# Storing x early and adding the attention output in DRAM, in a two-layer graph kernel on one core

## The chip, the cores and the metric

The kernel runs on one core of one Trainium2 chip. The metric is the device time of one execution in microseconds (us). The engines are PE (matrix products; PEld is its weight load), DVE (vector), ACT (scalar), POOL (GpSimd) and SP, which here only issues transfers. All arrays are float32.

## What is computed

x is 128 batches of 128 nodes with 512 features. Two residual layers follow each other; each normalizes x over its features, takes the positive part (called h), and adds the layer's output to x:

```python
    h = jnp.maximum(_layernorm(x, axis=-1), 0.0)
    x = x + _L0_gnn_ref(h, adj, ...)   # q k^T times adj^T, rows divided by their norm, times v
    h = jnp.maximum(_layernorm(x, axis=-1), 0.0)
    x = x + _L1_gnn_ref(h, adj, ...)   # 8 heads of 64, masked softmax attention, with biases
```

The second residual add is what the change moves: x after layer 0 plus the attention output of layer 1.

## The kernel before, in words

**Groups.** The 128 batches are worked in 32 groups of 4. Layer 0 of a group, layer 1's first part and layer 1's rest lie in different turns of the loop, so that three groups are in work at once: in a turn, `m` is layer 0 of the current group, `n` is the start of layer 1 of the same group (normalization and turning), `l` is layer 1 of the group before, `p` is the last part of layer 1 of the group before that, and `f` is the start of layer 0 of the next group.

**Order.** Nothing is scheduled by a tool. The strings FIRST, SECOND, ORDER and LAST list the steps by hand ("n.hn1" is step `hn(1)` of `n`); `run` calls them in turn, and each engine executes its instructions in the order in which they were issued. FIRST and SECOND are for the first two groups, ORDER for the other 30, LAST for what is left behind the last one. A step that waits on one engine holds up everything behind it on that engine.

**Products.** The 512x512 products go by a seven-product scheme for 2x2 blocks (class `Product`, steps P1 to P7, line 229 for all matrix instructions). Four PSUM banks serve them (`ps_mm`). ACT or DVE copies a bank out (`keep`, `copy`), DVE adds it to what was kept (`add`, line 253) and with that frees it. The sums of blocks of h, `s[0]` to `s[3]`, are made by DVE (`sumA`, `sumB`, lines 367 to 372).

**Turning through DRAM.** h, the softmax weights and the attention output have to be turned (features to partitions). ACT writes them to SBUF in blocks and issues one transfer to a DRAM scratch (`send_blocks`, line 195: `d_h`, `d_w`, `d_o`); SP issues four transfers that fetch the blocks back in another order (`fetch_blocks`, line 203: `u_h`, `u_w`, `u_o`); DVE finishes with a transpose of 32x32 blocks (lines 324, 510, 649). For h of layer 1 the steps are `n.inv` (POOL, lines 301 to 304, from DVE's statistics), `n.hn` (ACT, line 312, and the send), `n.rd` (fetch), `n.T` (DVE, line 324), each for half a group (two batches); the sums and the products `pq_*`, `pk_*` of queries and keys follow.

**x.** Each batch's x is a tile of 256 KB, `xb`, out of a pool of 12. It is loaded by POOL's queue (`load`, line 70) a group ahead, gets layer 0's output by DVE (line 439), is read for layer 1's h, and is kept until layer 1's output comes: in `p.ot0` and `p.ot1`, for two batches each, DVE turns the output into `o` (two buffers) and divides it by the softmax sums (line 654), POOL adds it to `xb` (line 661) and issues the store to the output (line 662). The loads `f.load0` to `f.load3` of a later group follow behind on POOL; a buffer is free when its store has landed. In the first group `w.loadx` loads the group after the next. The last group, 31, ends by itself in `fin` (lines 587 to 604), which adds and stores batch by batch.

## Time and profile before

| what | value |
|---|---|
| time, median of 3 runs | 2489.65 us (2489.06 to 2491.18) |
| profiled execution, its own time | 2488.91 us |
| its span, first to last instruction | 2487.1 us |
| granted clock | 1.0 |
| busy DVE, ACT, POOL | 1724.2, 1027.0, 531.0 us |
| DMA, mean | 405.72 MB, 163 GB/s |
| HBM read, written | 204.80 MB, 198.18 MB |
| POOL's adds, line 661 | 124 x 1274 ns |
| POOL's loads and stores of x | 124 and 124, 256.0 KB each |

How to read it: "busy" is the time in which an engine has an instruction in work. "Idle before, and releaser" says what the engine waited for. "a <- b" names the tile written and the tiles read, without numbers: `u_h<-d_h` is a fetch of h from the scratch. "us, times, longest" are the three numbers of a wait. A DMA share of 1 is all 16 transfer engines at work. The names with q (SPq, ACTq, POOLq) are the queues that issue transfers.

### The profile page before, as it was taken

What the parts mean: (1) busy time and instruction counts of PE and PEld (TensorE: products, weight loads), DVE (VectorE), ACT (ScalarE), POOL (GpSimd) and SP (SyncE); (2) the same over time, 40 slices, a digit from 0 to 9 for tenths busy, and PEclk for the clock granted to TensorE, in tenths of its full rate; (3) what the DMA queues carried; (4) which work ended last, traced back from release to release, by engine and by line L of the source; (5) the groups of instructions that cost most, each with busy time, mean ns of one, the idle gap of its engine ahead of it and who ended that gap; (6) DMA issues with size and microseconds to landing.
All of it is one profiled execution on the core that took longest, in us unless ns stands there. A gap on an engine that the chain in (4) does not pass through costs nothing.

```text
span 2487.1 us, 40880 instructions
## 1 busy us (share of the span) xinstructions
PE 2479.4 (100%) x14688; PEld 2114.3 (85%) x14688; DVE 1724.2 (69%) x2549; ACT 1027.0 (41%) x3248; POOL 531.0 (21%) x944
## 2 busy tenths in 40 slices
PE   9999999999999999999999999999999999999999
PEld 7888888888888888888888888888888888888888
DVE  5666776667766677766677666776667776667766
ACT  3344443444433444434444344443344443343434
POOL 5111222122212212122122211221211212212111
PEclk9999999999999999999999999999999999999999
DMA  6256554565644556445555455554455644555544
GB/s 202 81 164 178 178 163 150 156 180 166 186 145 147 179 169 193 145 146 168 178 178 162 150 155 182 166 180 148 147 174 173 189 144 145 176 175 181 153 131 141
DMA packets 370619, 405.72 MB, mean 163 GB/s; under 512 B 29616, under 2 KB 287024, under 8 KB 370416
## 3 DMA queue, kind: packets, MB, share of 16 engines
q1 hardware_dynamic: 279520, 168.71, 26.4%
q10 hardware_dynamic: 70000, 165.96, 18.4%
q0 software_dynamic: 20896, 68.44, 8.4%
q8 instruction: 116, 1.90, 0.3%
q14 instruction: 87, 0.71, 0.1%
HBM read 204.80 MB, written 198.18 MB: 162 GB/s over the span
## 4 chain that ended last, share of the span: by engine, by line
PE 94%; DMA 2%; DVE 2%; issue 1%; SPq 1%; ACT 0%; POOL 0%; ACTq 0%; DVEq 0%; POOLq 0%
PE pv_x L229 16%; PE pg_x L229 9%; PE pq_x L229 8%; PE pk_x L229 8%; PE pv_z L229 8%; PE pg_z L229 5%; PE pr L393 5%; PE pq_z L229 5%; PE po L626 4%; PE pk_z L229 4%; PE pv_y L229 4%; PE po L433 4%; PE pss L471 4%; PE pg_y L229 2%; PE pq_y L229 2%; PE pk_y L229 2%
## 5 line engine op out<-in xcount | busy, mean ns | idle before, releaser
L661 POOL TENSOR_TENSOR xb<-xb,o 128x512 f32<-128x512 f32 x124 | 158.0, 1274 | 1175.2 <-DVE o L654 1157.4
L229 PE MATMUL pv_x<-wc_v,h 128*128 128x256 f32 x1280 | 300.8, 382 | 0.7 <-DVE pv_r L246 0.7
L229 PEld LDWEIGHTS pv_x<-wc_v,h 128*128 128x128 f32 x1280 | 240.4, 190 | 51.6 <-issue 20.0
L229 PE MATMUL pv_z<-wc_v,s 128*128 128x256 f32 x1024 | 245.1, 382 | 0.0
L324 DVE STREAM_TRANSPOSE h<-u_h 128x1024 f32<-128x1024 f32 x126 | 156.5, 1242 | 113.6 <-DMA u_h<-d_h 112.0
L312 ACT ACTIVATE hn<-xb,shift,rstd 128x512 f32<-128x512 f32 x252 | 191.0, 807 | 74.4 <-POOL shift L304 57.2
L229 PEld LDWEIGHTS pv_z<-wc_v,s 128*128 128x128 f32 x1024 | 191.9, 190 | 28.7
L495 ACT ACTIVATE e<-pss,nmax 128x128 f32<-128x128 f32 x504 | 177.7, 384 | 38.9 <-DVE nmax L488 38.9
L229 PE MATMUL pv_x<-wc_v,s 128*128 128x256 f32 x768 | 181.7, 379 | 0.0
L229 PE MATMUL pq_x<-h,wc_q 128*128 128x256 f32 x768 | 181.5, 379 | 0.0
L229 PE MATMUL pk_x<-h,wc_k 128*128 128x256 f32 x768 | 181.5, 379 | 0.0
L637 ACT COPY oT<-po 128x512 f32<-128x512 f32 x124 | 72.7, 586 | 259.6 <-PE po L626 196.2
L294 DVE BATCH_NORM_STATS2 st<-xb 128x6 f32<-128x512 f32 x256 | 171.9, 672 | 8.7 <-DMA xb<-in_x_dram 8.7
L229 PEld LDWEIGHTS pq_x<-h,wc_q 128*128 128x128 f32 x768 | 145.8, 190 | 19.9
L229 PEld LDWEIGHTS pk_x<-h,wc_k 128*128 128x128 f32 x768 | 145.8, 190 | 19.9
L510 DVE STREAM_TRANSPOSE wT<-u_w 128x1024 f32<-128x1024 f32 x126 | 152.8, 1213 | 9.4 <-DMA u_w<-d_w 8.1
L229 PEld LDWEIGHTS pv_x<-wc_v,s 128*128 128x128 f32 x768 | 143.3, 190 | 18.4 <-issue 0.2
L301 POOL TENSOR_SCALAR rstd<-mv 128x2 f32<-128x2 f32 x128 | 28.4, 222 | 478.1 <-DVE mv L295 475.7
L654 DVE TENSOR_TENSOR o<-o,rs 128x512 f32<-128x512 f32 x124 | 124.3, 1003 | 4.3
L229 PE MATMUL pg_z<-s,wc_a 128*128 128x256 f32 x512 | 124.1, 385 | 0.0
L229 PE MATMUL pq_z<-s,wc_q 128*128 128x256 f32 x512 | 121.8, 381 | 1.4 <-DVE qT L253 1.2
L626 PE MATMUL po<-wT,v 128*64 128x128 f32 x1984 | 122.0, 276 | 0.0
(157 smaller groups left out, 4839.0 us busy)
## 6 DMA issues: line engine op xcount, KB each, us to landing
d_h<-hn ACTq DMA_DIRECT2D x126, 512.0 KB, 4.2
u_h<-d_h SPq DMA_DIRECT2D x504, 128.0 KB, 3.8
d_w<-e ACTq DMA_DIRECT2D x126, 512.0 KB, 3.0
u_w<-d_w SPq DMA_DIRECT2D x504, 128.0 KB, 3.3
xb<-in_x_dram POOLq DMA_DIRECT2D x124, 256.0 KB, 3.1
d_o<-oT ACTq DMA_DIRECT2D x62, 512.0 KB, 3.7
u_o<-d_o SPq DMA_DIRECT2D x248, 128.0 KB, 3.2
out_dram<-xb POOLq DMA_DIRECT2D x124, 256.0 KB, 3.0
```

What stands on the lines that cost most here:

```text
L229: nc.tensor.matmul(ps[:, m, :], lhsT=lhsT, rhs=rhs, start=first and m == 0 and k == 0, stop=k == 1, skip_group_check=True,)
L294: nc.vector.bn_stats(st, x_tiles[g, b])
L312: nc.scalar.activation(hn[:, r], x_tiles[g, b].rearrange("p (k j q) -> p j k q", j=TB, q=BK), AF.Relu, bias=self.shift[:, b : b + 1], scal ...
L324: nc.vector.transpose(half.rearrange("p k (t i) -> p t k i", i=BK), self.u.pop(i).rearrange("p t (k q) -> p t k q", q=BK),)
L393: nc.tensor.matmul(pr[:, b, :], lhsT=self.turned(k, b), rhs=self.gT[:, k, ts(b, P)], start=(k == 0), stop=(k == KD - 1),)
L433: nc.tensor.matmul(po, lhsT=self.rel[:, b, :], rhs=self.v[:, b, :], start=True, stop=True)
L471: nc.tensor.matmul(half[r][:, k, :], lhsT=self.qT[rows, k, ts(b, P)], rhs=self.kT[rows, k, ts(b, P)], start=True, stop=True,)
L495: nc.scalar.activation(e[:, :, i, :], sc[:, i, :].rearrange("p (j q) -> p j q", q=BK), AF.Exp, bias=nmax[:, i : i + 1], accum_out=self.tot ...
L510: nc.vector.transpose(self.wT[b].rearrange("p h (t i) -> p t h i", i=BK), self.uw.pop(b).rearrange("p t (h q) -> p t h q", q=BK),)
L626: nc.tensor.matmul(po[r * HD : (r + 1) * HD, k, :], lhsT=self.v[:, b, ts(2 * k + r, HD)], rhs=wT[:, r * NH + k, :], start=True, stop=True,)
L654: nc.vector.tensor_tensor(heads, heads, self.rs.pop(b).rearrange("p (r k) -> p k r", r=2)[:, :, :, None].to_broadcast([P, NH, 2, HD]), ALU ...
L661: nc.gpsimd.tensor_tensor(xb, xb, o.rearrange("p k t q -> p (k t q)"), ALU.add)
```

## The change

A layer-1 half's x is stored to the output as soon as its h is sent off, and its buffer is then free; the attention output goes to the same place later by a transfer that adds to what is there, from `o` and not from `xb`. POOL's add goes. The pool of x has 8 buffers. `w.loadx` is taken out of FIRST, so group 2 is loaded by `f.load` in SECOND. In LAST, `l.V.P6` (a product on PE and its eviction by DVE, line 246) stands ahead of `l.mx2` (DVE's maximum of the scores) instead of behind the exponentials. PE, ACT and SP have the same instructions in the same order as before; DVE has one pair exchanged, in LAST.

```diff
-    xpool = ctx.enter_context(tc.tile_pool(name="xpool", bufs=12))
+    xpool = ctx.enter_context(tc.tile_pool(name="xpool", bufs=8))
...
             self.d[i] = send_blocks(hn.rearrange("p n j k q -> p n j (k q)"), 2, f"h{n}_{g}_{i}")
+            if n and g < NG - 1:
+                for b in range(2 * i, 2 * i + 2):
+                    nc.gpsimd.dma_start(out[g * G + b], x_tiles.pop((g, b)))
...
                 b = 2 * i + n
-                xb = x_tiles.pop((g, b))
                 o = work.tile([P, NH, TB, BK], F32, tag="o", name=f"o_{g}_{b}")
...
-                nc.gpsimd.tensor_tensor(xb, xb, o.rearrange("p k t q -> p (k t q)"), ALU.add)
-                nc.gpsimd.dma_start(out[g * G + b], xb)
+                nc.gpsimd.dma_start(out[g * G + b], o.rearrange("p k t q -> p (k t q)"), accum_op=ALU.add)
...
-        w.scale m.G.P3 m.V.P1 f.hn1 f.rd1 w.sumv w.loadx m.G.P7 m.V.P2 w.sumq m.G.P4 m.V.P5
+        w.scale m.G.P3 m.V.P1 f.hn1 f.rd1 w.sumv m.G.P7 m.V.P2 w.sumq m.G.P4 m.V.P5
...
-        l.start_v l.V.P1 l.mkB1 l.exD1 l.wr1 l.V.P2 l.wt0 l.V.P5 l.S2 l.S3 l.add_mask2 l.mx2 l.exA2 l.exB2 l.V.P6
+        l.start_v l.V.P1 l.mkB1 l.exD1 l.wr1 l.V.P2 l.wt0 l.V.P5 l.S2 l.S3 l.add_mask2 l.V.P6 l.mx2 l.exA2 l.exB2
```

In the changed kernel the line numbers are 3 higher from line 317 to 646, 2 higher from there to 660 and 1 higher behind that: the turn of h is line 327, the eviction line 256, the early stores line 319, the accumulating transfer line 663.

## The prediction, as it was put on record

> **What bounds the kernel now.** I read the page first, then PE's waits, then what stands before the products that read the sums, then one group in time with PE's neighbours.

> The page's first part and PE's own list of waits:

> ```profile
> PE 2479.4 (100%) x14688; PEld 2114.3 (85%) x14688; DVE 1724.2 (69%) x2549; ACT 1027.0 (41%) x3248; POOL 531.0 (21%) x944
> ```
> ```profile
> PE idle L123 <- POOL ident masks.py:199: 1.4, 1, 1.4
> PE pq_z L229 <- DVE qT L253: 1.2, 2, 0.9
> PE pv_x L229 <- DVE pv_r L246: 0.7, 1, 0.7
> PE pg_x L229 <- ACT pg_r L237: 0.2, 1, 0.2
> ```

> PE is busy 2479.4 of 2487.1 us and waits 3.5 us in all. POOL and DVE work that is taken away gives nothing back unless PE waits for it, so there is at most 3.5 us to gain. What can be lost is open. So the question is how little spare time PE has, and where. The tile view of the sums (`s`) lists the idle time before their readers, weight loads included:

> ```profile
>   DVE qT L253: 5.5, 12
> ```

> Twelve times the load ahead of `pq_z` stood until DVE's eviction L253 was done. That place is on the edge in a good part of the 32 groups. In time, in the group around 1280 us (rows of the timeline, others left out):

> ```profile
> 1269.13 2.04 SPq L203 DMA_DIRECT2D u_h<-d_h  x4
> ...
> 1269.66 0.19 POOL L304 TENSOR_TENSOR shift<-shift,rstd 128x2 f32<-128x2 f32 x1
> 1269.71 0.33 ACTq L195 DMA_DIRECT2D d_w<-e  x1
> ...
> 1271.71 0.38 ACTq L195 DMA_DIRECT2D d_h<-hn  x1
> ...
> 1276.10 2.06 SPq L203 DMA_DIRECT2D u_h<-d_h  x4
> ...
> 1278.07 0.38 ACTq L195 DMA_DIRECT2D d_o<-oT  x1
> ...
> 1282.13 1.25 DVE L324 STREAM_TRANSPOSE h<-u_h 128x1024 f32<-128x1024 f32 x1 [1.20 <-DMA u_h<-d_h]
> ...
> 1284.74 0.68 DVE L253 TENSOR_TENSOR qT<-pq_y,pq_r 128x512 f32<-128x512 f32 x1
> ...
> 1286.08 1.24 PE L229 MATMUL pq_z<-s,wc_q 128*128 128x256 f32 x5
> ```

> This is layer 1's second half, `n.hn1`, `n.rd1`, `n.T1`: out to DRAM, back, turned by DVE, which sat 1.20 us for the fetch. Four DVE instructions later (turn, two sums, L253) PE starts `pq_z`. Spare time here: 1286.08 - 1285.42 = 0.66 us. I made the same subtraction in the timelines of groups 0 to 30: 0.05 to 0.32 in 14 of them (1.85 us together), 0.61 to 0.97 in 7 (5.43), 1.01 to 1.78 in 10 (12.76). The mean is 0.65 us, and in 28 of the 31 DVE waits for `u_h` just before the turn. **A fetch that comes later by D costs PE the sum of D minus spare, wherever that is positive.** For D of 0.8, 1.2, 1.6, 2.0 and 2.6 us that is 10, 18, 30, 42 and 61 us.

> How full the transfers are in that stretch (columns: window, sum, busy of PE, weight load, DVE, ACT, POOL, clock, DMA share, GB/s):

> ```profile
> 1270.00:1271.00 1.00, 1.00 (x6) 0.89 (x5) 0.56 (x1) 0.84 (x2) 0.00 (x0) 1.00 0.54 163
> 1271.00:1272.00 1.00, 1.00 (x6) 0.88 (x5) 1.00 (x2) 0.68 (x1) 0.00 (x0) 1.00 1.01 353
> 1272.00:1273.00 1.00, 1.00 (x7) 0.87 (x6) 0.96 (x3) 0.00 (x0) 0.00 (x0) 1.00 0.99 369
> 1273.00:1274.00 1.00, 1.00 (x6) 0.90 (x5) 0.85 (x3) 0.00 (x0) 0.52 (x2) 1.00 1.04 246
> 1274.00:1275.00 1.00, 1.00 (x12) 0.67 (x13) 0.24 (x1) 0.00 (x0) 0.83 (x3) 1.00 1.00 368
> ```

> From 1271 to 1275 all 16 engines are full: a fetch, the weights going out and `d_h`. The mean DMA share of the page (4 to 6 tenths) hides this.

> **The change, part by part.**

> *Stores at `n.hn0` and `n.hn1`*: four POOL issues a group, 31 groups, 256 KB each. Engine time of one: POOL's queue (page, part 3) moved 68.44 MB in 8.4% of the span, 208.9 us, which is 0.80 us for 256 KB; two are **1.6 us** of all 16 engines. Issue to data: the store issued at 1246.01 moves in the window 1247 to 1248. The instruction order of the changed kernel puts the stores right behind the four POOL operations of `inv`, without a new wait on a compute engine. For `hn1` these end at 1269.85, so the data flow from about 1271.0: into the full stretch, ahead of `d_h` (issued 1271.71). For `hn0` they end at 1264.72 and the stores move at 1265.9 to 1267.4, where the DMA share is near nothing; I cost these at nothing. If that cover were gone, `n.T0` would come 1.6 us later, and has about 3 us (turn done 1276.01, `pq_x` at 1279.17).

> D for the `hn1` stores: 1.6 us put into a full stretch go straight onto `d_h`, the fetch behind it cannot start before `d_h` has landed, and from 1276 to 1281 the share is 0.86 to 1.08 again. Lower end: all that is free between 1270 and 1281 (0.46 + 0.32 + 0.06 + 0.14, about 1.0) takes some in, D = 0.6 and 7 us. Upper end: the fetch, pushed back, now meets `d_o` (issued 1278.07, 512 KB, 1.4 us by the ACT queue's 18.4% for 165.96 MB) and loses about 1.0 more, D = 2.6 and 61 us. I take **D = 1.6, +30 us**, the work itself, as free time and the meeting with `d_o` about cancel.

> [...] Here the contention is between transfers, and PE pays through DVE's wait.

> *POOL's adds L661 go* (124 x 1274 ns = 158 us) and with them POOL's wait of 83.0 us for its own stores before the loads L70. Neither is in PE's list: 0. DVE's second multiply L654 of a pair takes 1.31 us beside the add and 0.69 without; 62 x 0.62 = 38 us of DVE, which lie ahead of Layer 0's turns, where PE does not wait: 0.

> *Accumulating transfers L663*: 124 instead of the plain stores, issued when DVE's `o` is done, some 2 us earlier. No row shows one. Lower bound: a plain store, 0.8 us. Upper bound: that all engines are held for the whole landing time of a POOL transfer, 3.1 us. Value: a store and a load, 1.6 us, since it reads and writes the output. [...] At `p.ot0` (1290 to 1301) two would add 1.6 us, and the loads come some 4 us earlier, another 1.6, ahead of Layer 0's fetches. Their spare time is larger: the end of the first turn stands 1.3 to 5.4 us, mean 4.0, ahead of `pg_x` (group at 1220: 1222.07 to 1225.07). So 3.2 us are covered nearly everywhere: 0 to 5 us in all, I take 0. At `p.ot1` (1244 to 1250) the DMA engines are empty by 1248. The buffer `o` is used again half a group later: no wait. Behind an accumulating issue POOL has only loads and statistics that are due tens of us later.

> *8 buffers of x*: a load now waits for the store of the group before, landed some 20 us earlier: 0. *`w.loadx` gone*: group 2 loads in SECOND, ahead of its statistics: 0.

> *Last group, V.P6 before mx2*: PE's 0.67 us before `pv_x` at 2470.31 goes (L246 starts 0.7 to 1.2 us sooner), but the reduce and the eight exponentials (2469.75 to 2472.56) come 0.68 later, and the transposes `pw` (2472.14 to 2473.18) read the last of them at once. Net -0.7 to +0.4: 0.

> Sum: profiled execution 2488.91 (span 2487.1 and 1.8 around it) + 30 = 2519; the median of the three runs is 0.7 higher, so 2520.

> **The rivals.**

> 1. *The stores are hidden anyway.* The free 1.0 us in the stretch, or POOL issuing a little sooner, lets them through; D stays under 0.5, stall under 5 us, not slower: 2486 to 2494. For it: the mean DMA share is near 0.5. Against: four full windows in a row. It decides where D falls under the spare time of the 14 tight groups, 0.3 us.
> 2. *The accumulating transfer is dear.* At 3.1 us each, two take 6.2 us for 1.6, and with the earlier loads Layer 0's fetch comes 6 us later against a spare 4.0: 2 us a group, 30 groups, +60 on top of 30: about 2580. For it: no row; against: nothing but the bounds.
> 3. *Faster*: PE's waits of 3.5 us are all there is, 2486 at best. It is not 0.2% (5 us).

> **How the numbers follow.** What a measurement here can tell from no change is about 0.2%, 5 us. Forecast (D about 0.9 to 2.6, 2500 to 2553) 0.64; D between (2495 to 2500) 0.06; rival 1 0.16; rival 2 0.12; faster 0.02. The range 2490 to 2565 leaves out most of rival 2 and the lower part of rival 1. Faster 0.02, same 0.16, slower 0.82.

> **What would show it.** In the changed profile PE's list should have `pq_z` <- DVE qT L253 (now with another line number) some 25 times and 20 to 60 us in all; DVE's idle before the second layer-1 turn should grow by D, POOL's wait for stores vanish, and written plus read bytes rise. If PE waits instead at `pg_x` or `pg_z`, rival 2 holds. If neither list grows, rival 1 does and I am wrong about the full stretch.

## The result, and the profile after

The changed kernel takes 2585.16 us (median of 4 runs, 2579.92 to 2589.01), the kernel before 2489.84 (4 runs, 2489.06 to 2491.18). The ratio is 1.0381, 95% interval 1.0362 to 1.0400: **95 us slower**. The forecast was 2520 in a range of 2490 to 2565: the sign was right, the size was three times as large. The profiled execution of the changed kernel took 2589.01 us, its span is 2587.2, its mean granted clock 0.991.

The page of the changed kernel: busy time of the engines, the queue of POOL (packets, MB, share of the 16 transfer engines), and the bytes.

```profile
PE 2501.7 (97%) x14688; PEld 2128.6 (82%) x14688; DVE 1685.4 (65%) x2549; ACT 1027.2 (40%) x3248; POOL 490.3 (19%) x944
...
q0 software_dynamic: 38752, 100.95, 16.3%
...
HBM read 204.80 MB, written 230.69 MB: 168 GB/s over the span
```

PE's own waits in the changed kernel (us in total, times, longest):

```profile
PE pv_x L229 <- DVE v L253: 73.5, 30, 4.1
PE pq_x L229 <- issue: 4.2, 1, 4.2
PE idle L123 <- POOL ident masks.py:199: 1.4, 1, 1.4
PE pv_z L229 <- DVE pv_r L246: 1.2, 1, 1.2
PE pg_x L229 <- ACT pg_r L237: 0.2, 1, 0.2
```

The balance is short. The span grew by 100.1 us. PE's waits grew from 3.5 to 80.5, which is 77.0. PE's busy time grew by 22.3 for the same 14688 instructions. Together 99.3. So there are two things to explain: a wait of about 2.5 us in each of 30 groups, at a place for which the forecast has no wait in these groups (`pv_x` behind DVE's `v`, not `pq_z` behind `qT`), and matrix products that take longer. DVE and POOL lost 38.8 and 40.7 us of work, and nothing came of it.

(The eviction by `add` kept its line number, 253, in the changed kernel: the "256" told before the prediction, and the prediction's "now with another line number", are wrong. In the lines of the second experiment, L330 is the turn of h, which is L327 in the changed kernel.)

**Where PE stands.** Rows of the timeline of the kernel before, DVE and PE around the first turn of layer 1, `n.T0`, in the same group that the prediction used (start, duration, instruction; in brackets the idle time before it):

```profile
1274.76 1.25 DVE L324 STREAM_TRANSPOSE h<-u_h 128x1024 f32<-128x1024 f32 x1 [0.88 <-DMA u_h<-d_h]
...
1275.93 0.65 DVE L253 TENSOR_TENSOR v<-pv_x,pv_r 128x512 f32<-128x512 f32 x1
...
1277.34 1.99 PE L229 MATMUL pv_x<-wc_v,h 128*128 128x256 f32 x8
...
1279.17 1.03 PE L229 MATMUL pq_x<-h,wc_q 128*128 128x256 f32 x4
```

ORDER has `l.V.P3 n.T0 l.V.P7`. The second row is P7's eviction of layer 1 of the group before, which stands behind the turn on DVE and has nothing to do with it. It frees the bank that PE's next product, `l.V.P4` (third row), writes to. It ends at 1276.58, and PE starts at 1277.34: **0.76 us to spare** (0.13 to 1.01 in the 31 groups that have this place, median 0.72). The prediction looked past it to the reader of the turned h itself, `pq_x` at 1279.17, and counted 3 us.

Rows of the timeline of the changed kernel, the same place in a group some 600 us later:

```profile
1876.81 1.18 POOL L319 DMA_DIRECT2D out_dram<-xb  x2
...
1878.38 0.38 ACTq L195 DMA_DIRECT2D d_h<-hn  x1
...
1881.59 2.40 SPq L203 DMA_DIRECT2D u_h<-d_h  x4
...
1881.79 0.33 ACTq L195 DMA_DIRECT2D d_w<-e  x1
...
1881.98 1.18 POOL L319 DMA_DIRECT2D out_dram<-xb  x2
...
1883.79 0.38 ACTq L195 DMA_DIRECT2D d_h<-hn  x1
...
1889.73 1.25 DVE L327 STREAM_TRANSPOSE h<-u_h 128x1024 f32<-128x1024 f32 x1 [3.78 <-DMA u_h<-d_h]
1890.90 0.65 DVE L253 TENSOR_TENSOR v<-pv_x,pv_r 128x512 f32<-128x512 f32 x1
...
1891.61 1.99 PE L229 MATMUL pv_x<-wc_v,h 128*128 128x256 f32 x8 [2.13 <-DVE v L253]
...
1896.03 1.25 DVE L327 STREAM_TRANSPOSE h<-u_h 128x1024 f32<-128x1024 f32 x1 [0.27 <-DMA u_h<-d_h]
```

(L319 is the early store; `x2` merges two issues.) Read it from the top. The stores of the first half (1876.81) go out before that half's h is sent (1878.38). The stores of the second half are issued at 1881.98, 0.4 us behind the *first* half's fetch (1881.59). The first turn begins 8.14 us behind its fetch's issue; before, in the group above, 5.63 (1269.13 to 1274.76). It is 2.5 us later, DVE sits 3.78 us for it instead of 0.88, the eviction behind it is late, and PE stands 2.13 us. The second turn, for which the prediction feared, waits 0.27 us only: PE has by then been pushed back, and all that is counted from PE has moved with it.

What moved meanwhile, by queue (packets, MB, share of 16 engines; the fetches are q1, the sends q10, POOL's q0), and the fetches' median time to landing (of the issues that lie in the window). Before, 1270 to 1275:

```profile
q10 hardware_dynamic: 366, 0.97, 52.8%
q1 hardware_dynamic: 1092, 0.53, 38.8%
...
u_h<-d_h SPq DMA_DIRECT2D x2, 128.0 KB, 4.2
```

After, 1882 to 1890:

```profile
q1 hardware_dynamic: 1538, 0.94, 43.4%
q10 hardware_dynamic: 416, 1.05, 35.7%
q0 software_dynamic: 160, 0.52, 16.2%
...
u_h<-d_h SPq DMA_DIRECT2D x3, 128.0 KB, 6.1
```

Both stretches are full (0.92 and 0.95 in sum). In the second, 0.52 MB are the two stores, 16.2% of 8 us = 1.3 us of all engines, and a fetch lands in 6.1 us instead of 4.2. Over all groups, the first half's fetch lands 8.2 us after its first issue instead of 5.5 (means of 31).

**Slower products.** The second part, 22.3 us of PE's busy time, is in the clock. The view by stretch of the changed kernel, after the wait at 1811 (columns: window, sum, busy of PE, weight load, DVE, ACT, POOL, clock, DMA share, GB/s):

```profile
1811.20:1812.50 1.30, 1.30 (x6) 1.17 (x7) 1.27 (x2) 0.00 (x0) 0.00 (x0) 0.95 1.00 289
1812.50:1815.90 3.40, 3.40 (x10) 2.69 (x9) 3.16 (x5) 2.34 (x14) 0.00 (x0) 0.52 0.63 129
1815.90:1819.30 3.40, 3.40 (x18) 2.99 (x17) 3.17 (x5) 2.81 (x8) 0.00 (x0) 1.00 0.88 279
```

and PE's rows there:

```profile
1811.18 2.65 PE L229 MATMUL pv_x<-wc_v,h 128*128 128x256 f32 x8 [2.26 <-DVE v L253]
1813.62 2.97 PE L229 MATMUL pq_x<-h,wc_q 128*128 128x256 f32 x8
1816.42 1.89 PE L229 MATMUL pq_y<-h,wc_q 128*128 128x256 f32 x8
```

PE waited, worked 1.3 us at nearly the full clock, and was then granted half of it for one stretch of 3.4 us: 10 matrix instructions instead of 18. I found 12 such stretches inside the changed kernel, each behind a wait, and none in the kernel before. The mean clock says the same: (1 - 0.991) x 2587 = 23 us of PE's work not granted, waits included; the 79 instructions that I found at half rate, at 0.216 us more each, make 17. By the profile's own clock record, 12 stretches of 3.413 us at half withhold 20.5 us.

### The profile page after: what moved, and what is told of

Same layout as the page of the kernel before. It is cut to its first block, busy times and chain, and to the rows that moved or that the text cites. A ratio compares the mean times of both kernels' runs of the same rounds, so it can differ in the third digit from the quotient of the medians.

```text
span 2587.2 us, 40707 instructions
## 1 busy us (share of the span) xinstructions
PE 2501.7 (97%) x14688; PEld 2128.6 (82%) x14688; DVE 1685.4 (65%) x2549; ACT 1027.2 (40%) x3248; POOL 490.3 (19%) x944
## 3 DMA queue, kind: packets, MB, share of 16 engines
q10 hardware_dynamic: 70000, 165.96, 17.2%
q0 software_dynamic: 38752, 100.95, 16.3%
HBM read 204.80 MB, written 230.69 MB: 168 GB/s over the span
## 4 chain that ended last, share of the span: by engine, by line
PE 79%; DMA 10%; DVE 4%; issue 3%; SPq 2%; POOL 1%; ACT 1%; DVEq 0%; ACTq 0%; POOLq 0%
PE pv_x L229 11%; PE pq_x L229 9%; PE pk_x L229 9%; PE pg_x L229 9%; DMA u_h<-d_h 6%; PE pv_z L229 5%; PE pg_z L229 4%; PE pr L396 4%; PE pq_z L229 4%; PE pk_z L229 4%; PE po L436 3%; PE pss L474 3%; PE pv_y L229 2%; PE po L629 2%; DMA d_h<-hn 2%
## 5 line engine op out<-in xcount | busy, mean ns | idle before, releaser
L663 POOL DMA_DIRECT2D out_dram<-o x124 | 111.4, 904 | 1444.6 <-DVE o L656 1396.0
L229 PE MATMUL pv_x<-wc_v,h 128*128 128x256 f32 x1280 | 311.7, 392 | 73.5 <-DVE v L253 73.5
L229 PEld LDWEIGHTS pv_x<-wc_v,h 128*128 128x128 f32 x1280 | 246.3, 195 | 128.2 <-DVE v L253 79.2
L327 DVE STREAM_TRANSPOSE h<-u_h 128x1024 f32<-128x1024 f32 x126 | 156.8, 1245 | 268.0 <-DMA u_h<-d_h 233.8
L229 PE MATMUL pv_z<-wc_v,s 128*128 128x256 f32 x1024 | 245.2, 382 | 1.2 <-DVE pv_r L246 1.2
L229 PEld LDWEIGHTS pv_z<-wc_v,s 128*128 128x128 f32 x1024 | 191.8, 190 | 30.2 <-DVE pv_r L246 1.6
L229 PE MATMUL pq_x<-h,wc_q 128*128 128x256 f32 x768 | 190.9, 393 | 4.2 <-issue 4.2
L229 PE MATMUL pv_x<-wc_v,s 128*128 128x256 f32 x768 | 181.7, 379 | 0.0
L229 PE MATMUL pk_x<-h,wc_k 128*128 128x256 f32 x768 | 181.5, 379 | 0.0
L229 PEld LDWEIGHTS pq_x<-h,wc_q 128*128 128x128 f32 x768 | 153.7, 200 | 28.3 <-issue 4.6
L229 PEld LDWEIGHTS pk_x<-h,wc_k 128*128 128x128 f32 x768 | 145.8, 190 | 19.9
L229 PEld LDWEIGHTS pv_x<-wc_v,s 128*128 128x128 f32 x768 | 143.3, 190 | 18.4 <-issue 0.2
L229 PE MATMUL pg_z<-s,wc_a 128*128 128x256 f32 x512 | 124.1, 385 | 0.0
L229 PE MATMUL pg_x<-s,wc_a 128*128 128x256 f32 x512 | 121.1, 379 | 0.2 <-ACT pg_r L237 0.2
L229 PE MATMUL pg_x<-h,wc_a 128*128 128x256 f32 x512 | 121.1, 379 | 0.1
L229 PE MATMUL pq_z<-s,wc_q 128*128 128x256 f32 x512 | 121.1, 379 | 0.0
```

The source lines that it names most:

```text
L229: nc.tensor.matmul(ps[:, m, :], lhsT=lhsT, rhs=rhs, start=first and m == 0 and k == 0, stop=k == 1, skip_group_check=True,)
L327: nc.vector.transpose(half.rearrange("p k (t i) -> p t k i", i=BK), self.u.pop(i).rearrange("p t (k q) -> p t k q", q=BK),)
L663: nc.gpsimd.dma_start(out[g * G + b], o.rearrange("p k t q -> p (k t q)"), accum_op=ALU.add)
```

## The experiments

The theories. **A**: the early stores, those of the second half above all, delay layer 1's fetches, and PE waits through DVE's order. **B**: the accumulating transfers, or the loads that come earlier with them, cost the time. Then, within A: which half, by how many bytes, and by which reader.

### Stores alone, without the adding transfers (e1_stores_only)

```diff
 (from the kernel before)
+            if n and g < NG - 1:
+                for b in range(2 * i, 2 * i + 2):
+                    nc.gpsimd.dma_start(out[g * G + b], x_tiles[g, b])
```

POOL's adds and the later stores stay; the same place is written again later.

> The kernel before, with the early stores of x at layer 1's h added and all else kept (POOL's add and its store afterwards, which writes the same place again; 12 buffers). Theory A, the early stores of the second half push the first half's fetch, DVE's turn of it stands ahead of the eviction of pv_x, and PE waits there: nearly the whole loss is here, 2560 to 2595 us, PE waiting for DVE v L253 about 30 times and 60 to 75 us. Theory B, the accumulating transfers cost the time: 2487 to 2500 us.

Measured: 2582.39 us, ratio 1.0374 (1.0359 to 1.0390), within 3 us of the changed kernel. PE's waits:

```profile
PE pv_x L229 <- DVE v L253: 73.6, 30, 3.8
```

The same wait to 0.1 us, and PE busy 2497.6. The stores alone make the whole loss. B falls for the changed kernel.

### All but the early stores (e2_late_stores)

```diff
 (from the changed kernel; xpool bufs=12)
-            if n and g < NG - 1:
+        def st(self, i):
+            g = self.g
+            if g < NG - 1:
...
 (ORDER; in SECOND l.st0 ahead of f.load2 and l.st1 behind f.load3)
-        ... m.sumB m.start m.G.P1 ...  f.load2 f.load3 m.R ...
+        ... m.sumB m.start l.st0 m.G.P1 ...  f.load2 f.load3 l.st1 m.R ...
```

The stores of x go out in the group's next turn, where no fetch of layer 1's h is in flight.

> The changed kernel with all early stores moved to two quiet places of the next turn (behind the start of layer 0 and behind the last load), with 12 buffers; the accumulating transfers stay. Theory A: 2487 to 2500 us, no wait of PE for DVE v L253. Theory B: 2560 to 2590 us.

Measured: 2513.85, ratio 1.0099 (1.0084 to 1.0114). PE's waits:

```profile
PE pg_x L229 <- DVE h L330: 10.4, 6, 2.8
PE pq_z L229 <- DVE qT L253: 5.6, 5, 4.1
```

The 73.5 us are gone (1.4 left at that place), so A holds for some 70 of the 95 us. But the kernel is 14 us over what A allowed: something else costs 25 us here. The wait at `pg_x` is what the prediction's second rival named. The last two experiments below take these 25 us apart.

### One half early, the other late (e3_first_early, e4_second_early)

```diff
 (from the changed kernel; xpool bufs=12; e3 has i == 0, e4 has i == 1; the other half by st as in e2)
-            if n and g < NG - 1:
+            if n and i == 0 and g < NG - 1:
```

> Only the first half's x is stored early (at hn0), the second half's in the quiet place behind the last load. Theory A: the first half's stores move in an empty stretch and delay its send by some 0.5 us, less than the 0.76 us that the eviction of pv_x had to spare: 2487 to 2505 us. Theory A2, that the first half's own stores delay its fetch: 2540 to 2590 us.

> Only the second half's x is stored early (at hn1), the first half's in the quiet place behind the start of layer 0. Theory A: nearly the whole loss, 2555 to 2590 us, PE waiting for DVE v L253 about 30 times by 2 us. Theory A2, that the first half's own stores do it: 2487 to 2515 us.

Measured: the first half early 2519.49 (1.0125, 1.0108 to 1.0141), above the range that A had for it, the second half early 2562.95 (1.0296, 1.0281 to 1.0312). PE's waits with the first half early, and with the second half early:

```profile
PE pv_x L229 <- DVE v L253: 6.6, 6, 3.2
```
```profile
PE pv_x L229 <- DVE v L253: 50.1, 30, 3.0
```

Against the kernel with all stores late, the first half's stores cost 5.6 us by themselves and the second half's 49. Both together make 71 (2585.16 - 2513.85), so the first half's cost 22 when they come on top, 17 more than alone: PE's wait goes from 50.1 to 73.5. The traces say why. With the first half early, its send lands in 3.2 us instead of 2.8 (means of 31 groups), so the fetch behind it is issued 0.4 us later. That fits into the 0.72 us to spare, unless the second half's stores have used it up. The forecast of "nothing" for the first half is near right alone and wrong in company.

### Half of the second half (e8_half_early)

```diff
 (from the changed kernel; xpool bufs=12; the other three batches by st)
-            if n and g < NG - 1:
-                for b in range(2 * i, 2 * i + 2):
+            if n and i == 1 and g < NG - 1:
+                nc.gpsimd.dma_start(out[g * G + 2], x_tiles.pop((g, 2)))
```

> As e4, but at hn1 only one of the two batches is stored early (256 KB for 512 KB); the other goes to the quiet place behind the last load. Theory A: the delay of the fetch falls by the 0.8 us of one store, PE's wait for DVE v L253 from 50.1 us to about 26: 2525 to 2548 us. If one early store is as bad as two (a fixed cost of having a third queue at work): 2555 to 2565 us.

Measured: 2534.47 (1.0185, 1.0168 to 1.0202).

```profile
PE pv_x L229 <- DVE v L253: 22.5, 27, 2.2
```

One store of 256 KB a group: 22.5 us of this wait; two: 50.1; four: 73.5. With none, 1.4. The fetch itself says the same: from its first issue to its landing it takes 5.6 us with none, 6.9 with one, 7.8 with two at `hn1` (means of 31 groups). So the delay grows with what moves beside the fetch, which a fixed cost of a third queue at work would not. Whether the bytes or the number of transfers count is not told apart here.

### The turn behind the eviction (e5_turn_behind, e6_before_turn_behind)

```diff
 (SECOND and ORDER; e5 from the changed kernel, e6 from the kernel before)
-        l.V.P3 n.T0 l.V.P7 l.S3 ...
+        l.V.P3 l.V.P7 n.T0 l.S3 ...
```

If PE stands because P7's eviction is queued on DVE behind a late turn, putting it ahead must take this wait away and leave the late turns to their own readers.

> The changed kernel, with one pair of steps exchanged in the two middle orders: DVE's turn n.T0 stands behind l.V.P7, so the eviction of pv_x no longer waits for the fetch. All transfers stay as they are. Theory A (the wait for the fetch is passed on to PE only through the eviction behind it): PE's wait for DVE v L253 goes from 73.5 us to under 10; the late fetch then shows at the next place, pq_z behind DVE qT, with 1.0 to 1.5 us a group: 2515 to 2545 us. Rival C, that PE is slowed by the load on DMA or memory itself: still 2570 to 2590 us.

> The same exchange in the kernel before. PE hardly waits there, so all theories: 2486 to 2491 us. It shows that the exchange by itself is worth nothing, and that e5 measures the wait.

Measured: 2553.73 (1.0270, 1.0255 to 1.0286), some 30 us less than the changed kernel; in the kernel before the same exchange does nothing, 2489.23 (1.0004, 0.9995 to 1.0013). PE's waits in the first:

```profile
PE pq_z L229 <- DVE qT L253: 36.4, 30, 2.4
PE pq_x L229 <- DVE h L327: 7.8, 12, 1.5
PE pq_x L229 <- issue: 4.1, 1, 4.1
```

A group of it in the timeline: the eviction, the two turns and the products behind them:

```profile
1702.26 0.69 DVE L253 TENSOR_TENSOR v<-pv_x,pv_r 128x512 f32<-128x512 f32 x1 [0.57 <-PE pv_x L229]
...
1705.14 1.99 PE L229 MATMUL pv_x<-wc_v,h 128*128 128x256 f32 x8
1705.23 1.25 DVE L327 STREAM_TRANSPOSE h<-u_h 128x1024 f32<-128x1024 f32 x1 [2.28 <-DMA u_h<-d_h]
...
1711.97 1.25 DVE L327 STREAM_TRANSPOSE h<-u_h 128x1024 f32<-128x1024 f32 x1 [1.31 <-DMA u_h<-d_h]
...
1714.58 0.68 DVE L253 TENSOR_TENSOR qT<-pq_y,pq_r 128x512 f32<-128x512 f32 x1
1715.32 1.99 PE L229 MATMUL pq_z<-s,wc_q 128*128 128x256 f32 x8 [1.28 <-DVE qT L253]
```

The eviction is now done at 1702.95, PE's `pv_x` follows without a wait, and no wait for `v` is left in PE's list. The turn is still late (DVE sits 2.28 and 1.31 us), and the next place on the edge takes it up: `pq_z` behind `qT`, 30 times, 36.4 us. That is the wait of the forecast, which had 30 us for it. It had been there all the time, behind a tighter one. The time missed the expected range by 9 us: of the 73.5 us taken away, 44.2 came back at the turns' own readers (36.4 and 7.8).

### The last group's exchange alone (e7_last_only)

```diff
 (from the kernel before, in LAST)
-        ... l.add_mask2 l.mx2 l.exA2 l.exB2 l.V.P6
+        ... l.add_mask2 l.V.P6 l.mx2 l.exA2 l.exB2
```

> The kernel before with only the exchange in LAST (l.V.P6 ahead of l.mx2). By the prediction's working -0.7 to +0.4 us: 2487.5 to 2490.5 us, no difference to be told. In its profile PE's 0.7 us before pv_x should be gone and a wait at the last transposes should have come in its place.

Measured: 2489.07 us against 2490.48, ratio 0.9996 (0.9987 to 1.0005). No difference that can be measured. The wait for `pv_r` (0.7 us) is gone from PE's list; its waits are 3.7 us in sum, as before (3.5). The wait that was expected in its place at the last transposes is not in the list; one at `pv_x` behind `v` is, 0.9 us in two times.

### Late stores without the adding (e9_plain_o)

```diff
 (from e2)
-  nc.gpsimd.dma_start(out[g * G + b], o.rearrange("p k t q -> p (k t q)"), accum_op=ALU.add)
+  nc.gpsimd.dma_start(out[g * G + b], o.rearrange("p k t q -> p (k t q)"))
```

This leaves out layer 1's residual add in all groups but the last: the attention output is written over x.

> As e2 (late stores, 12 buffers), but the attention output is stored plainly over x and not added to it, so the residual add of layer 1 is left out for all groups but the last. It tells what the adding itself costs. If the 25 us that e2 still lost come from the adding transfers' double work: 2488 to 2500 us. If they come from the stores moved to the quiet places or from the earlier loads: 2508 to 2518 us, as e2.

Measured: 2496.79 (1.0036, 1.0023 to 1.0049), 17 us less than with the adding. POOL's queue in the profile of the late stores with the adding, and without it (packets, MB, share):

```profile
q0 software_dynamic: 38752, 100.95, 16.3%
```
```profile
q0 software_dynamic: 30816, 100.95, 11.7%
```

The same count of transfers and the same MB. 16.3% of 2515.3 us is 410.0, 11.7% of 2493.4 is 291.7: 118.3 us over 124 transfers, 0.95 us more for each that adds, on top of 291.7/372 = 0.78 for a plain one. With the adding gone, the waits at `pg_x` (10.4 us) are gone too, and PE's busy time falls from 2489.2 to 2480.8. So 17 of the 25 us of the late stores are the adding, felt at layer 0's fetches and in the clock (0.996 in e2's profiled execution, 0.999 in e9's). POOL's issue also shortens, from 904 to 565 ns; that the transfers' own work does it, and not this, is likely by its size and not shown.

### The load of group 2 in its old place (e10_late_loadx)

```diff
 (from e2; in FIRST, and in SECOND)
-        ... f.hn1 f.rd1 w.sumv m.G.P7 ...
+        ... f.hn1 f.rd1 w.sumv w.loadx m.G.P7 ...
-        ... f.stat3 f.inv1 m.V.P6 ...
+        ... f.stat3 f.inv1 l.st0 l.st1 m.V.P6 ...
```

The kernel with late stores has, near the start, one wait of 4.08 us (row of its timeline):

```profile
77.96 3.78 PE L229 MATMUL pq_z<-s,wc_q 128*128 128x256 f32 x8 [4.08 <-DVE qT L253]
```

There POOL issues group 2's loads and group 0's stores from 61.4 to 66 us, beside the sending and fetching of group 0's second half. In the kernel before the loads went out at 43.9. The edit moves both, the loads ahead and the stores behind.

> As e2 (late stores, 12 buffers, adding transfers), with w.loadx back in FIRST and group 0's stores behind f.inv1 of SECOND, where POOL has to wait. In e2 POOL ran ahead and issued group 2's loads and group 0's stores at 61 to 66 us, amid the fetch of group 0's second half, and PE waited 4.1 us at pq_z. If that is the cause: this wait goes and the time is 4 us below e2, 2508 to 2511 us. If the wait at 78 us stays, the loads were not its cause.

Measured: 2509.26 (2501.86 to 2513.0; ratio 1.0066, 1.0050 to 1.0081), 4.6 us less than the late stores. All of PE's waits at `pq_z` are now 0.7 us together. The median agrees with the price of the wait; the four runs are 11 us apart and the kernel before took 2490.48 beside them, 2488.22 beside the late stores, so the time by itself does not prove it. In the changed kernel a wait of 4.2 us stands at `pq_x` and 72 us, where group 0's early stores and then group 2's loads go out from 61.8 us on. With the stores alone (e1), where the loads go out at 42.9, it is:

```profile
PE pq_x L229 <- issue: 1.6, 1, 1.6
```

So of the 4.2 us, 1.6 are there without the moved loads, and 2.6 come with them.

## Why the prediction was right and wrong

**Right: the question.** PE is the bound, DVE's and POOL's savings are worth nothing, and the price is what a late fetch costs PE beyond its spare time. DVE gave back 38.8 us (38 forecast), POOL's 83.0 us of waiting for its own stores vanished, and PE gained nothing from either.

**Wrong: which fetch the stores of `hn1` delay, and what a late first turn costs.** The step is the end of the part on the stores: "I cost these at nothing. If that cover were gone, `n.T0` would come 1.6 us later, and has about 3 us (turn done 1276.01, `pq_x` at 1279.17)". Two faults meet there.
- The spare time was read at the wrong reader. I went from the turn to those who read its result. The instruction that hurts reads nothing of it: it is only next in DVE's queue. The rule told ahead of the prediction, that a step which waits holds up everything behind it on its engine, was applied to the second turn and not to the first. The spare time was 0.76 us and not 3, and the exchange in e5 shows that this row is the one that counts.
- The stores of `hn1` were charged to the second half's path alone (`d_h`, then its fetch). They are issued 0.4 us behind the first half's fetch and move beside it, and alone they cost 50.1 us at `pv_x` (e4). The forecast had "a fetch" among the transfers of the full stretch, and asked only what is late behind it, not that this fetch itself becomes late.

So the mechanism (stores in a full stretch make a fetch late, DVE's turn waits, PE waits for an eviction behind it) was right, with the wrong fetch and the wrong eviction: 73.5 us at `pv_x` in place of 30 at `pq_z`. The sign the prediction named, more idle time of DVE before the second turn, did not come: it fell from 1.07 to 0.39 us (means of 31 groups).

**Nearly right: the size of the forecast's own term.** With the first place out of the way (e5) PE waits 36.4 us at `pq_z`, against +30, 30 times, against some 25. That is in another order of steps and with all four stores, so it bears the term out without measuring it alone.

**Missing: the clock.** The sum took each wait at its own length. 12 waits were followed by a stretch at half the clock, some 20 us in all. Of the 30 waits at `pv_x`, all five of 3.6 us or more were followed by half the clock, and of the 25 shorter ones (1.9 to 2.9 us) six were too. The twelfth is the wait of 4.2 us at 72 us. What sets them apart in this trace is told in the last section.

**Accumulating transfers: cost right, effect half right.** 1.6 us of all engines was forecast for one; by the queue's share it is 0.78 + 0.95 = 1.73 in e2, and in the changed kernel (421.7 - 208.9)/124 = 1.72. A plain one takes 0.78 to 0.80 by the queue's share here, so the ratio is some 2.2. The share also holds some 3.4 MB of other transfers. Taken from the packets themselves (2 KB for one that adds, 4 KB for a plain one), an adding transfer takes 1.77 us in e2 and 1.82 in the changed kernel, a plain one 0.71 to 0.79, so the ratio is 2.3 to 2.5. "In all, I take 0" holds in the changed kernel, where the stores already push PE back: it and e1 are 3 us apart. Where PE is on time (e2 against e9) it is 17 us, at `pg_x`, as rival 2 said, at a quarter of its price. That rival's 2580 is near the measured time by accident: PE hardly waits at `pg_x` in the changed kernel.

**`w.loadx` gone, at nothing: 2.6 us.** The loads of group 2 moved into a stretch where group 0's h is fetched (4.2 us of wait in the changed kernel against 1.6 in e1; the 8 buffers are the other difference there). I had asked only when the loads are needed, not what they meet.

**8 buffers, the exchange in LAST: nothing**, as forecast for the exchange (e7); the buffers were not tried by themselves, and e1, with 12, leaves at most 3 us for them and all else.

**Bytes:** written HBM bytes rose by 32.51 MB, which is 124 x 256 KB; the count of read bytes did not change (204.80 MB in both). That an adding transfer reads the output back was the prediction's estimate; the page's counter does not show it.

**What stays open.** In six groups (at 378, 775, 1174, 1572, 1971 and 2368 us, every fifth) the wait is 2.9 to 4.1 us instead of about 2.2. In all six, and in one other group, a packet of 16 KB of the profile's `instruction` queue starts 3.8 to 5.7 us behind the fetch's issue and takes 0.9 to 1.5 us. That fits a fetch that lands at 8.9 to 10.0 us instead of about 8, but no run here tests it. Of the 25 us of e2, 17 and 4.6 are accounted for, some 4 are not. Of PE's 22.3 us more of busy time, the clock record has 20.5 and the rest is not explained. No version here beats the kernel before; PE waits 3.5 us in it, and e6 and e7 equal it.

## What to carry to other kernels

When an instruction will be late on an engine that works in order, list everything behind it in that engine's queue, and take the spare time at the first whose reader is the bounding engine, whether or not it reads the late data. When a transfer is moved into a full stretch, price it against every transfer in flight there, the ones issued just ahead of it first. And where the bounding engine has no idle time, a moved transfer can only lose: work taken off POOL and DVE bought nothing here, while 512 KB a group at the wrong moment cost 1.6 us a group (49 us in e4).
